# Attention values of two consecutive steps mixed together and summed in one PSUM bank

## The chip, the core and the metric

The kernel runs on one core of a Trainium2 chip. The metric is the device time of one execution in microseconds (us). Engines are named as the profile names them: PE is TensorE (its weight loads are PEld), DVE is VectorE, ACT is ScalarE, POOL is GpSimd, SP is SyncE. PE writes its results to PSUM, which has 8 banks; a bank holds 512 fp32 numbers for each of 128 partitions. DVE and ACT read PSUM, POOL does not.

## The reference

The program is a small network on 2 sequences of 1024 tokens with 256 features, all in fp32: a first attention with 16 heads of 16 features, a soft mixture of 64 experts, a rotation of the features, and two layers of a local-window attention with a gated feed-forward part. The change lies wholly in the first attention, which is this part of the reference:

```
qkv = (x @ Wqkv.T + bqkv).reshape(Bb, Ss, 3, H, HD).transpose(2, 0, 3, 1, 4)
q, k, v = (qkv[0], qkv[1], qkv[2])
attn = softmax(einsum('bhid,bhjd->bhij', q, k) / sqrt(HD), axis=-1)
...
out = einsum('bhij,bhjd->bhid', mod, v)       # mod is attn, gated and renormalised
```

For each of 2 x 16 heads, 1024 queries meet 1024 keys. The kernel computes exp(score - maximum), multiplies it with the values and with a column of ones (which gives the sum), and divides at the end.

## The kernel before

**Units and steps.** Four heads of one sequence form a unit; there are 8 units (`units`). A unit is worked off in 16 steps, 128 steps in all (`STEPS`). Step s belongs to unit s // 16, to one half n of the queries (512) and to one block j of 128 keys: j runs from 0 to 7, then n changes. Three kinds of work make up the loop at L767:

- `maxima(step, half)` (L301): the maximum of each query over the keys must be known before its exponentials. For two heads at a time ("half" 0 and 1), two matmuls with 32 contraction rows each fill a tile `pm` of two banks, and DVE reduces it to maxima (L317). This runs `LEAD` = 12 steps ahead of the scores, so that there are maxima for steps 12 to 127 in loop steps 0 to 115 and none in the last 12 loop steps. `largest` and `shift` turn the maxima of 8 steps around and put them into the queries (`qs`) of the next half unit.
- `score(step, half)` (L336): two matmuls with 32 contraction rows give the scores of two heads, each in a bank of its own (`sc`), and ACT takes the exponential into an SBUF tile `e` (L352). In the last 12 steps half 1 uses one tile of two banks and one exponential.
- `mix(s)` (L355): four matmuls, one a head, with 128 contraction rows (keys) and 32 output rows each, multiply the values `v` of step s with the four exponentials. The four results stand one under the other in one bank, `po`. For j = 0 ACT copies `po` to an SBUF tile `ob` (L373). For the other j the result is added to `ob`: ACT copies `po` to `part` (L379) and POOL adds (L380), or, from step 116 on, DVE adds straight from PSUM (L376).

An fp32 matmul is two passes, so that one matmul of the program is two MATMUL records of the profile: a loop step has 8 records of scores, 8 of maxima and 8 of mixing. The four matmuls of a mix lie in four column strips of the array and run side by side. Scores and maxima lie in four row strips: the scores of one half and the maxima of the other half run side by side.

**Order of the work.** PE, DVE and ACT take their instructions in the order in which the program is written here (`manual_schedule`). A loop step is: `largest` (on some even steps), the mix of two steps earlier, `shift` and the list `between` (on odd steps only: projections, transposes and the like), then score half 0 with maxima half 1, maxima half 0 with score half 1, and last the list `aside` (small DVE work). This document calls the two score-and-maxima pairs of one step its *block*.

**PSUM.** The 8 banks are two pools. `ps_s` has two buffers of two banks; in the loop only `pm` uses them (and, in the last 12 steps, the wide score tile). So the `pm` of a step can be written once DVE has reduced the `pm` of the same place in the step before. `ps_t` has four buffers of one bank, taken in turn by `po`, the four `sc` of a step, and whatever `between` needs. The exponentials `e` have 6 buffers, two a step.

At the end, `mix(126)` and `mix(127)` are written into the beginning of the next stage, after its first logits.

Of the kernel before, what the change touches and what calls it, by code (L numbers as in the profile page):

```python
# [91 lines left out]
def tile_kernel(ctx: ExitStack, tc: tile.TileContext, a: dict, out: bass.AP):  # L92
    nc = tc.nc
# [51 lines left out]
    at = ExitStack()  # L145
# [21 lines left out]
    VW = HD0 + 1  # L167
    v = [at1.tile([P, 8, H0 * VW + 32 - VW], F32, name=f"v{b}") for b in range(B)]
# [18 lines left out]
    def single(name):  # L187
        return ps_t[0].tile([P, 512], F32, tag="t", name=name)
# [130 lines left out]
    def largest(hu):  # L319
        mx2 = mxs.pop(hu)  # L320
        nc.vector.tensor_tensor(mxt[hu % 2][:, :, :, AUG], mx2[:, :, :, 0], mx2[:, :, :, 1], ALU.max)

    def shift(hu):

        u, n = divmod(hu, 2)
        pt = one("pmx")
        for i in range(4):
            nc.tensor.transpose(
                pt[:, i * P : (i + 1) * P], mxt[hu % 2][:, i, :, :].rearrange("p h r -> p (h r)"), ident
            )  # L330
        at = slice(n * 512, (n + 1) * 512)
        nc.vector.tensor_tensor(qs[u % 2][:, at], qm[u % 2][:, at], pt, ALU.add)

    es = {}

    def score(step, half):  # L336

        u, n, j = step // 16, step % 16 // 8, step % 8
        e = at2.tile([P, 2, 512], F32, tag="e", name="e", bufs=6)
        both = half and step >= STEPS - LEAD  # L340
        sc = wide("sc") if both else [single("sc") for x in range(2)]
        for x in range(2):
            r = slice(32 * (2 * half + x), 32 * (2 * half + x) + 32)
            nc.tensor.matmul(  # L344
                sc[:, x, :] if both else sc[x],
                km[u % 3][r, j * P : (j + 1) * P],
                qs[u % 2][r, n * 512 : (n + 1) * 512],
                start=True,
                stop=True,
            )  # L350
        for part, t in ((e, sc),) if both else ((e[:, x, :], sc[x]) for x in range(2)):
            nc.scalar.activation(part, t, AF.Exp, scale=1.0 / HD0**0.5)  # L352
        es[step, half] = e

    def mix(s):  # L355

        u, n, j = s // 16, s % 16 // 8, s % 8
        b, g = units[u]
        po = single("po")
        for hh in range(4):  # L360
            at = (4 * g + hh) * VW
            nc.tensor.matmul(  # L362
                po[32 * hh : 32 * hh + 32, :],
                v[b][:, j, at : at + 32],
                es[s, hh // 2][:, hh % 2, :],
                start=True,
                stop=True,
            )
        for x in range(2):
            es.pop((s, x))  # L370
        if j == 0:
            obs[u, n] = at2.tile([P, 512], F32, tag="ob", name=f"ob{u}_{n}")
            nc.scalar.copy(obs[u, n], po)  # L373
            return
        if s >= STEPS - LEAD:
            nc.vector.tensor_tensor(obs[u, n], obs[u, n], po, ALU.add)  # L376
            return
        part = at2.tile([P, 512], F32, tag="part", name="part", bufs=1)
        nc.scalar.copy(part, po)  # L379
        nc.gpsimd.tensor_tensor(obs[u, n], obs[u, n], part, ALU.add)  # L380
# [34 lines left out]
    def add_field(b, n, which=range(4)):  # L415
        o_tm = o_tms[b]
        for i in (4 * n + y for y in which):
            nc.vector.scalar_tensor_tensor(
                o_tm[:, i, :], sv[b], fac[:, b * 8 + i : b * 8 + i + 1], o_tm[:, i, :], ALU.mult, ALU.add
            )  # L420
# [27 lines left out]
    def out_by_token(b, n):  # L448
        for i in range(4):
            t0 = 1 + (4 * n + i) * P  # L450
            if i % 2 == 0:
                pt = one("pxt").rearrange("p (y d) -> p y d", d=D)
            for c in range(2):
                nc.tensor.transpose(pt[:, i % 2, c * P : (c + 1) * P], xa[:, c, b, t0 : t0 + P], ident)
            if i % 2:
                i0 = b * 8 + 4 * n + i - 1
                nc.vector.tensor_copy(xo_tm[:, i0 : i0 + 2, :], pt)
# [4 lines left out]
    STEPS = 16 * len(units)  # L462
# [253 lines left out]
    def of_banks(bufs):  # L716
        banks.close()
        ahead.clear()
        single_banks[0] = bufs == 4
        ps_t[0] = banks.enter_context(tc.tile_pool(name="ps_t", bufs=bufs, space=PSUM))  # L720
# [10 lines left out]
    for u in range(len(units)):  # L731
        if u % 2 == 0 and u + 2 < len(units):
            b, g = units[u + 2]
# [30 lines left out]
    with tc.manual_schedule(  # L764
        engines={mybir.EngineType.PE, mybir.EngineType.DVE, mybir.EngineType.Activation}
    ):
        for s in range(STEPS):  # L767
            u, p = s // 16, s % 16 // 2
            new = p in (3, 7) and s // 8 + 1 < 2 * len(units)
            if new and s % 2 == 0:  # L770
                largest(s // 8 + 1)
            if s >= 2:
                mix(s - 2)
            if s % 2:
                if new:
                    shift(s // 8 + 1)
                for f in between.get((u, p), ()):
                    f()
            m = s + LEAD
            for what in (0, 1) if m < STEPS else (0,):  # L780

                for f, step in ((score, s), (maxima, m))[:: 1 - 2 * what]:
                    if step < STEPS:
                        f(step, what if f is score else 1 - what)
            if m >= STEPS:
                score(s, 1)
            for f in aside.get(s, ()):
                f()
# [18 lines left out]
    def logits(it):  # L807

        n, m = divmod(it, 8)
        lg = wide("lg")  # L810
        for b in (1, 0):
            for k in range(2):
                nc.tensor.matmul(  # L813
                    lg[:, b, :],
                    xa[:, k, b, 1 + m * P : 1 + (m + 1) * P],
                    phi[:, k, n * 512 : (n + 1) * 512],
                    start=(k == 0),
                    stop=(k == 1),
                )
        keep = dx0.tile([P, B, 512], F32, tag="keep", name="keep")  # L820
        nc.scalar.copy(keep[:, 1, :], lg[:, 1, :])  # L821
        l1 = dx0.tile([P, 512], F32, tag="l1", name="l1")
        nc.vector.tensor_tensor(l1, lg[:, 0, :], keep[:, 1, :], ALU.subtract)  # L823
        nc.vector.tensor_copy(keep[:, 0, :], lg[:, 0, :])
        for b in range(B):
            nc.sync.dma_start(lgd[b * 8 + m][:, n * 512 : (n + 1) * 512], keep[:, b, :])
        dsps[it] = dx0.tile([P, B, 512], F32, tag="dsp", name="dsp")
        nc.scalar.activation(dsps[it][:, 0, :], l1, AF.Sigmoid)
        nc.scalar.activation(dsps[it][:, 1, :], l1, AF.Sigmoid, scale=-1.0)

    def dispatch(it):

        n, m = divmod(it, 8)
        if m == 0:
            accs[n] = [pair(f"sl{b}") for b in range(B)]
        d = dsps.pop(it)
        for b in range(B):
            for c in range(2):
                nc.tensor.matmul(  # L839
                    accs[n][b][:, c, :],  # L840
                    xo_tm[:, b * 8 + m, c * P : (c + 1) * P],
                    d[:, b, :],
                    start=(m == 0),
                    stop=(m == 7),
                )
        if m == 7:
            slots[n] = dx.tile([P, 2, B, 512], F32, tag="slots", name="slots", bufs=1)
            nc.scalar.copy(slots[n][:, :, 0, :], accs[n][0])
            nc.vector.tensor_copy(slots[n][:, :, 1, :], accs[n][1])
# [110 lines left out]
    with tc.manual_schedule(  # L960
        engines={mybir.EngineType.PE, mybir.EngineType.DVE, mybir.EngineType.Activation}
    ):
        logits(0)
        out_by_token(1, 0)
        mix(STEPS - 2)
        mix(STEPS - 1)
        of_banks(2)
        logits(1)
        by_token(len(units) - 1, 1)
        dispatch(0)  # L970
        add_field(1, 1)
        to_features(1, 1)
        logits(2)
        dispatch(1)
        project_out(1, 1)
        logits(3)
        dispatch(2)
        out_by_token(1, 1)
# [6 lines left out]
    y = [mo1.tile([P, NE // 4, D], F32, name="y0"), xp.tile([P, NE // 4, D], F32, tag="y1", name="y1")]  # L985
# [106 lines left out]
    with tc.manual_schedule(  # L1092
# [10 lines left out]
        ts, nrqs, vs, es, eTs, pos, oTs, hcs, us = {}, {}, {}, {}, {}, {}, {}, {}, {}  # L1103
# [455 lines left out]
        for s in range(-2, WINDOWS):  # L1559
# [73 lines left out]
            if s == 5:  # L1633

                f = xp.tile([P, 4 * NS], F32, tag="e", name="f")
                at = 0
# [159 lines left out]
```

## Time and profile before

| | us |
|---|---|
| median of 3 timed runs (1587.48 to 1588.11) | 1587.85 |
| span of the profiled execution, first to last instruction | 1586.1 |
| the same execution: time outside the span | not in the profile |
| loop step 0 begins (first score) | 63.2 |
| last mix ends, about | 499.6 |
| busy PE / DVE / ACT / POOL, whole span | 1572.0 / 904.2 / 892.3 / 538.6 |

The profile has a page of totals and groups, and a trace that can be asked for a list of instructions in order of time, for groups of instructions, for waits, and for the chain of work that ended last. In the list in order of time, a row has start, duration, engine, line, operation, tiles, shape, how many instructions are merged into the row, and in brackets the idle time of that engine before it and what ended it. A duration of a merged row runs from its first start to its last end. The ends of matmuls are modelled and overlap the next ones, so that the pace of PE is read from the starts. A wait that the profile puts down to an engine that had long been done was another's.

### The profile page before, as it was taken

The numbers are of one execution on the slowest core, as the hardware profiler recorded it, in microseconds if no ns is written. First come the engines' busy times: TensorE is split into PE (matmuls) and PEld (weight loads), VectorE is DVE, ScalarE is ACT, GpSimd is POOL, SyncE is SP. The second block draws the span as 40 slices with busy tenths as digits, with TensorE's granted clock in tenths as the row PEclk, the third lists the DMA queues.
The fourth block names the chain that finished last, engine by engine and source line by source line (L and its number), as shares of the span: only waits on it lengthen the run. The fifth ranks groups of instructions, "written<-read, shape, count | busy, mean of one in ns | idle before, by whom it ended". The sixth has DMA issues, their size and how long they took to land.

```text
span 1586.1 us, 22717 instructions
## 1 busy us (share of the span) xinstructions
PE 1572.0 (99%) x8672; PEld 801.4 (51%) x8672; DVE 904.2 (57%) x1606; ACT 892.3 (56%) x1678; POOL 538.6 (34%) x835
## 2 busy tenths in 40 slices
PE   8999999999999999999999999999999999999999
PEld 4333433333333444444887676555555555556554
DVE  5868768776863122225446656756565656656532
ACT  2578778787885222235234544666666565666641
POOL 3333323333330100000103444655554555465411
PEclk9999999999999999999999999999999999999999
DMA  5100010000000644546642002000100001000001
GB/s 161 54 15 13 1 21 8 8 14 8 1 1 34 172 152 139 184 149 185 204 130 77 30 1 82 1 1 1 67 1 0 14 1 56 1 11 17 14 14 40
DMA packets 49852, 82.66 MB, mean 52 GB/s; under 512 B 4552, under 2 KB 25200, under 8 KB 49488
## 3 DMA queue, kind: packets, MB, share of 16 engines
q1 hardware_dynamic: 47200, 75.38, 15.5%
q0 software_dynamic: 1584, 5.29, 1.1%
q8 instruction: 68, 1.11, 0.3%
q10 hardware_dynamic: 960, 0.56, 0.1%
q14 instruction: 40, 0.33, 0.1%
HBM read 56.04 MB, written 20.97 MB: 49 GB/s over the span
## 4 chain that ended last, share of the span: by engine, by line
PE 98%; DVE 1%; DMA 1%; ACT 0%; POOL 0%; issue 0%; ACTq 0%; DVEq 0%; POOLq 0%
PE sc L344 9%; PE pga L1412 9%; PE po L362 8%; PE pm L310 7%; PE lg L813 7%; PE pq L1140 7%; PE sl L839 7%; PE cmb L928 7%; PE py L1439 4%; PE po L1323 4%; PE sc L1243 4%; PE pwo L1343 3%; PE pe L1304 3%; PE pv L1210 3%; PE pqk L280 2%; PE py L860 2%
## 5 line engine op out<-in xcount | busy, mean ns | idle before, releaser
L317 DVE TENSOR_REDUCE mx<-pm 128x2 f32<-128x1024 f32 x256 | 301.6, 1220 | 108.0 <-PE pm L310 107.9
L352 ACT ACTIVATE e<-sc 128x512 f32<-128x512 f32 (+1 forms) x500 | 263.6, 613 | 67.7 <-PE pm L310 63.5
L344 PE MATMUL sc<-qs,km 32*128 32x512 f32 x1024 | 247.7, 616 | 0.7 <-ACT cg L562 0.7
L310 PE MATMUL pm<-km,qm 32*128 32x512 f32 x1024 | 242.8, 616 | 0.0
L380 POOL TENSOR_TENSOR ob<-ob,part 128x512 f32<-128x512 f32 x101 | 128.5, 1272 | 251.2 <-ACT part L379 251.2
L1412 PE MATMUL pga<-hc,w 128*128 128x512 f32 x320 | 141.8, 593 | 0.0
L1293 POOL TENSOR_SCALAR e<-e,den 128x256 f32<-128x256 f32 (+1 forms) x128 | 130.8, 1035 | 29.4 <-DVE den L1289 29.4
L362 PE MATMUL po<-e,v 128*32 128x512 f32 x1024 | 136.8, 604 | 0.0
L344 PEld LDWEIGHTS sc<-qs,km 32*128 32x128 f32 x1024 | 91.5, 183 | 86.6 <-ACT e L352 65.2
L1178 POOL TENSOR_TENSOR t<-raw,tabs 128x512 f32<-128x512 f32 x64 | 80.7, 1281 | 152.4 <-ACT raw L1170 147.2
L1277 ACT ACTIVATE e<-e,nmx 128x256 f32<-128x256 f32 (+1 forms) x256 | 123.5, 487 | 2.7 <-DVE nmx L1260 2.5
L1140 PE MATMUL pq<-wqo,xa 128*128 128x512 f32 x256 | 115.9, 595 | 1.1 <-ACT xa L955 0.7
L928 PE MATMUL cmb<-xb,y 128*128 128x256 f32 x512 | 116.5, 380 | 0.2 <-ACT xb L914 0.2
L813 PE MATMUL lg<-phi,xa 128*128 128x512 f32 x256 | 116.1, 595 | 0.0
L839 PE MATMUL sl<-dsp,xb 128*128 128x512 f32 x256 | 114.9, 592 | 0.0
L310 PEld LDWEIGHTS pm<-km,qm 32*128 32x128 f32 x1024 | 83.2, 183 | 49.3 <-DVE mx L317 35.0
L1260 DVE CUSTOM_DVE_ANT_0 e<-sc,mask,zn 128x256 f32<-128x256 f32 (+1 forms) x256 | 102.0, 463 | 6.3 <-PE sc L1243 6.3
L823 DVE TENSOR_TENSOR l<-lg,keep 128x512 f32<-128x512 f32 x32 | 22.1, 692 | 144.8 <-ACT keep L821 144.8
L928 PEld LDWEIGHTS cmb<-xb,y 128*128 128x128 f32 x512 | 95.0, 190 | 16.2 <-issue 2.8
L1170 ACT COPY raw<-pq 128x1024 f32<-128x1024 f32 x32 | 32.4, 1013 | 108.0 <-PE pq L1140 100.0
L1412 PEld LDWEIGHTS pga<-hc,w 128*128 128x128 f32 x320 | 59.0, 190 | 66.6 <-issue 64.3
L821 ACT COPY keep<-lg 128x512 f32<-128x512 f32 x32 | 18.7, 585 | 126.0 <-issue 105.3
(225 smaller groups left out, 2460.5 us busy)
## 6 DMA issues: line engine op xcount, KB each, us to landing
lgd<-keep SPq DMA_DIRECT2D x64, 256.0 KB, 2.4
w<-in_ffn_W SPq DMA_DIRECT2D x16, 1024.0 KB, 7.0
ebig<-lgd SPq DMA_DIRECT2D x64, 256.0 KB, 3.3
wqo<-in_wqkv SPq DMA_DIRECT2D x2, 1536.0 KB, 8.0
w<-in_w SPq DMA_DIRECT2D x2, 1386.0 KB, 5.9
km<-hk SPq DMA_DIRECT2D x32, 64.0 KB, 2.3
qm<-hq SPq DMA_DIRECT2D x32, 64.0 KB, 2.3
phi<-in_phi SPq DMA_DIRECT2D x1, 2048.0 KB, 7.7
```

The costliest lines, as they stand in the source:

```text
L310: nc.tensor.matmul(pm[:, x, :], qm[u % 2][r, i * P : (i + 1) * P], km[u % 3][r, n * 512 : (n + 1) * 512], start=True, stop=True,)
L317: nc.vector.tensor_reduce(mxs[hu][:, i % 4, 2 * half : 2 * half + 2, n], pm, AX.X, ALU.max)
L344: nc.tensor.matmul(sc[:, x, :] if both else sc[x], km[u % 3][r, j * P : (j + 1) * P], qs[u % 2][r, n * 512 : (n + 1) * 512], start=True, s ...
L352: nc.scalar.activation(part, t, AF.Exp, scale=1.0 / HD0**0.5)
L362: nc.tensor.matmul(po[32 * hh : 32 * hh + 32, :], v[b][:, j, at : at + 32], es[s, hh // 2][:, hh % 2, :], start=True, stop=True,)
L380: nc.gpsimd.tensor_tensor(obs[u, n], obs[u, n], part, ALU.add)
L813: nc.tensor.matmul(lg[:, b, :], xa[:, k, b, 1 + m * P : 1 + (m + 1) * P], phi[:, k, n * 512 : (n + 1) * 512], start=(k == 0), stop=(k == 1),)
L839: nc.tensor.matmul(accs[n][b][:, c, :], xo_tm[:, b * 8 + m, c * P : (c + 1) * P], d[:, b, :], start=(m == 0), stop=(m == 7),)
L928: nc.tensor.matmul(acs[q][:, c, :], y[b][:, 4 * jj + j, c * P : (c + 1) * P], eT[:, j // 2, j % 2 * 256 : (j % 2 + 1) * 256], start=(jj == ...
L1140: nc.tensor.matmul(pq[:, x, :], shifted(xa, k, b, w * WIN, P), load["wqkv"][:, k, x * 512 : (x + 1) * 512], start=(k == 0), stop=(k == 1),)
L1293: engine.tensor_scalar(e[:, x, c, lo:], e[:, x, c, lo:], den[:, x, c : c + 1], None, ALU.mult)
L1412: nc.tensor.matmul(pt[:, x, :], load["w1"][:, k, lo : lo + P], hcs[f][:, k, :], start=(k == 0), stop=(k == 1))
```

## The change

`mix(s)` is called for an even s only, in the odd loop step s + 3, and handles steps s and s + 1: eight matmuls instead of four, of which the second four add to the first four in the same bank (`start` only for the first step, `stop` for the second). One copy, or one copy and one addition, then serves both steps. Even loop steps have no mix. The line numbers after L358 grow by one.

```diff
         po = single("po")
-        for hh in range(4):
-            at = (4 * g + hh) * VW
-            nc.tensor.matmul(
-                po[32 * hh : 32 * hh + 32, :],
-                v[b][:, j, at : at + 32],
-                es[s, hh // 2][:, hh % 2, :],
-                start=True,
-                stop=True,
-            )
-        for x in range(2):
-            es.pop((s, x))
+        for y in range(2):
+            for hh in range(4):
+                at = (4 * g + hh) * VW
+                nc.tensor.matmul(
+                    po[32 * hh : 32 * hh + 32, :],
+                    v[b][:, j + y, at : at + 32],
+                    es[s + y, hh // 2][:, hh % 2, :],
+                    start=(y == 0),
+                    stop=(y == 1),
+                )
+            for x in range(2):
+                es.pop((s + y, x))
         if j == 0:
...
             if new and s % 2 == 0:
                 largest(s // 8 + 1)
-            if s >= 2:
-                mix(s - 2)
+            if s >= 3 and s % 2:
+                mix(s - 3)
             if s % 2:
...
         mix(STEPS - 2)
-        mix(STEPS - 1)
         of_banks(2)
```

## The prediction

> **What bounds the kernel now.** I read the page's totals first, then its groups, then the list in order of time at two places in the loop, then the chain that ended last.
>
> ```profile
> PE 1572.0 (99%) x8672; PEld 801.4 (51%) x8672; DVE 904.2 (57%) x1606; ACT 892.3 (56%) x1678; POOL 538.6 (34%) x835
> ...
> PE 98%; DVE 1%; DMA 1%; ACT 0%; POOL 0%; issue 0%; ACTq 0%; DVEq 0%; POOLq 0%
> ...
> L317 DVE TENSOR_REDUCE mx<-pm 128x2 f32<-128x1024 f32 x256 | 301.6, 1220 | 108.0 <-PE pm L310 107.9
> ```
>
> PE is busy 99% and makes 98% of the chain, so the time is PE's. But busy time is modelled, and what paces PE must be read from its starts. DVE's reductions are the next thing to look at: 256 of 1.22 us, two a loop step, each waiting for PE. The ordinary loop, from the list in order of time (from the mix of step 19 to that of step 20):
>
> ```profile
> 133.62 1.06 PE L362 MATMUL po<-e,v 128*32 128x512 f32 x8
> 134.62 0.70 PE L344 MATMUL sc<-qs,km 32*128 32x512 f32 x2
> ...
> 135.35 0.19 PEld L310 LDWEIGHTS pm<-km,qm 32*128 32x128 f32 x2 [0.42 <-DVE mx L317]
> ...
> 135.88 2.36 DVE L317 TENSOR_REDUCE mx<-pm 128x2 f32<-128x1024 f32 x2 [0.42 <-PE pm L310]
> ...
> 136.55 1.06 PE L362 MATMUL po<-e,v 128*32 128x512 f32 x8
> ```
>
> A mix takes 1.00 us to the next start (133.62 to 134.62), a block of scores and maxima 1.93 (to 136.55), a step 2.93. The mix of step 21 starts at 139.47, so that two steps are 5.85. DVE starts on a block's maxima 1.26 after the block begins and needs 2.36 for its two tiles: it ends 3.62 after the block's start. The second `pm` of the next block needs the buffer that is freed then. The next block starts at 2.93 and wants that buffer 0.97 into it (134.62 to 135.59 is the start of its second half), at 3.90. So the slack against DVE is only 0.3 us, less the load's own lead, and the mix is what provides it. The row at 135.35 shows that this load was released by DVE.
>
> Now a place where the loop of before has no mix between two blocks: steps 0 and 1, since the mix begins at step 2.
>
> ```profile
> 63.22 0.70 PE L344 MATMUL sc<-qs,km 32*128 32x512 f32 x2 [0.70 <-ACT cg L562]
> ...
> 64.48 4.81 DVE L317 TENSOR_REDUCE mx<-pm 128x2 f32<-128x1024 f32 x4 [1.43 <-PE pm L310]
> ...
> 65.03 0.29 PEld L344 LDWEIGHTS sc<-qs,km 32*128 32x128 f32 x2 [0.64 <-ACT e L352]
> ...
> 65.52 0.29 PEld L344 LDWEIGHTS sc<-qs,km 32*128 32x128 f32 x2 [0.20 <-ACT e L352]
> ...
> 66.89 0.19 PEld L310 LDWEIGHTS pm<-km,qm 32*128 32x128 f32 x2 [0.83 <-DVE mx L317]
> ...
> 67.96 1.06 PE L362 MATMUL po<-e,v 128*32 128x512 f32 x8
> ```
>
> Step 0's block starts at 63.22, step 1's at 65.03, 1.82 later. Its second score waits for a `sc` bank until 65.52, and its second `pm` waits for DVE until 66.89. DVE began at 63.22 + 1.26, as in the ordinary loop, and ended those two tiles at + 3.62; PE went on 0.05 later. The mix comes at 67.96: two blocks back to back take 4.74, not twice 1.93. This is the pattern that the change makes of every pair of steps.
>
> **The change part by part.**
>
> *Work removed.* ACT's copies to `part` fall from 101 to 43 (58 x 0.59 = 34 us), POOL's additions likewise (58 x 1.27 = 74 us), DVE's additions at L376 from 11 to 5 (6 x 0.69 = 4 us). Matmuls, exponentials, reductions and every DMA keep their number. I cost the removed work at nothing: it lies beside PE. ACT idles 63.5 us before its exponentials, waiting for PE, and what waited for `part` or for `ob` on PE are a handful of rows of up to 0.8 us, the length that PE also shows at each change from blocks to mixes. It also buys nothing at the wait above, which is on DVE's reductions, and those have 1201 to 1226 ns throughout, whatever POOL does beside them.
>
> *Mixes joined.* Within one kind of work a pass follows the last by 0.43 (eight passes of the projection in 3.44). Two passes of a mix should take 0.86 and take 1.00; four of a block should take 1.72 and take 1.93. So a change of kind and back costs 0.14 + 0.21, by finer starts 0.34 a step, and an even step without a mix saves it. Where two mixes stand together today, after the loop, the chain shows what a joined one costs:
>
> ```profile
> 482.42 1.00 PE po L362 x8
> ...
> 497.84 1.85 PE po L362 x16
> ```
>
> That is 1.85. Summing in PSUM costs no extra: the coherence product at L552 sums eight matmuls in the same four column strips at 0.43 to 0.45 a pass.
>
> The Trainium skill's "TensorEngine Tiling (Array Packing)" says in its section on tiling modes that a change of mode drains the array. By that rule alone the change would remove a drain pair from 57 even steps, and with the 0.34 of the rows the sum would be -19 us. Its section on the PSUM bottleneck warns the other way, that packed matmuls outrun what empties PSUM, but gives no price. The rows at 63 to 68 us decide between the two.
>
> *The cover that is lost.* With the mix gone from the even step, PE reaches that step's second `pm` at 1.82 + 0.86 = 2.68 after the odd block's start, and DVE frees it at 3.62 + 0.05 = 3.67. Once it is freed, 1.07 pass until the next mix (66.89 to 67.96). Unstalled, two blocks would be 1.82 + 1.93 - 0.11 (no change of kind before the second) = 3.64; they are 4.74. The stall is 1.10 us. What queues behind the waiting load on PE are the two scores of half 1 and then the joined mix; nothing on PE can pass it. ACT then gets half 1's scores late and idles, which costs nothing more: the next block's scores reuse banks whose exponentials ended long before.
>
> *Sum for a pair.* 1.85 + 4.74 = 6.59 against 5.85: +0.74, which is -0.34 for the changes of kind and +1.10 for the stall, within rounding. It holds for even steps 4 to 114, 56 of them, because in every odd step before 116 DVE starts at 1.26 and ends at 3.62, whatever stands in `between` (that is ahead of the block, and DVE's small work there ends before 1.26). 56 x 0.74 = 41.4. In the next odd block nothing is late: DVE ended 69.29 - 63.22 = 6.07 after the pair's first block, 1.8 before it is needed again. The `po` bank is reused by the last score of the odd block; today the copy starts 0.19 after the block (134.81 against 134.62), lasts 0.59, and that score starts at 0.98, so this stays as it is.
>
> *Step 2.* Blocks 0, 1 and 2 now follow each other. Block 2's second `pm` waits for DVE's 69.29; with 0.05 and 1.07 the joined mix starts at 70.41 and ends at 72.26. Today the mix of step 1 starts at 70.89 and ends at 71.89. +0.4.
>
> *The last twelve steps.* There are no maxima, so no DVE stall. Today a step is about 2.07 (mixes at 463.27 and 465.34). A joined mix needs the exponentials of the odd step two before, with one block between: they end about 3.2 after their scores, and PE is there at 1.93. The mix's first half covers 0.86 of that. I estimate 4.2 a pair against 4.13, and at the step that carries a `shift` a gain, since today's mix at 467.47 stretches to 1.39. Bounds for six pairs: -2 (PE alone, 3.78 a pair) and +5 (0.8 more wait each). I take 0, near which both estimates lie.
>
> *Waits that could be new.* `e` has 6 buffers; step s writes what step s - 3 left, whose mix still precedes step s's scores on PE. No new wait. `by_token` and `gate_outputs` read `ob` two or more steps after its last mix, as before. SP's and POOL's DMA issues are not moved past anything.
>
> *Total.* 41.4 + 0.4 + 0 = 41.8 on the span of 1586.1: 1627.9. The profile gives no time outside the span; the median 1587.85 stands 1.75 above it, and I keep that: **1629.7 us**, +2.6%.
>
> **The rivals.**
>
> 1. *The changes of kind decide* (other side, faster). If DVE's tile were free in time, 57 x -0.34 = -19 us, 1568. For it: PE is 99% busy, and its busy time falls. Against it: steps 0 and 1 show the stall itself. It decides only if DVE ended a block's maxima 1.0 us sooner, at 2.6; two reductions of 1.22 after 1.26 cannot. 5%, with all that lies between no change and it.
> 2. *More is late than in steps 0 and 1.* These had no copy of `po` on ACT and no bank taken by `po`. If the copy delayed the odd block's last score by its whole length, 0.59 a pair, 57 of them would add 34: 1663. Against it is the timing of the copy above. 8%, mostly for smaller amounts of the same kind.
> 3. *The change does little*: the stall and the saving cancel because other waits in the ordinary loop already contain the stall. The ordinary loop's block is 1.93 in all but three steps, so there is none to cancel. 2%.
>
> **How the numbers follow.** The case above has 85%. Its own range: 0.70 to 0.79 a pair gives 39 to 44, the tail -2 to +5: 1625 to 1637. Rival 2's smaller amounts reach up, a partly hidden stall down; I give 1620 to 1640 for eight in ten. A change under 0.2% (3.2 us), about what a measurement of this kernel can tell, counts as the same. Faster 5%: rival 1. Same 2%: rival 3. Slower 93%.
>
> **What the profile after would show.** Mixes as rows of 16 records, 1.85 to the next start, 6.59 apart where `between` is empty. In every even step a PE load of `pm` released by DVE, with about 0.8 idle before it, and DVE's reductions in runs of four, 4.8 long. `part` copies 43. PE's matmul groups unchanged in number. The waits of `pm` on DVE grow from 30 us to some 60 or more. Everything after 540 us is the old profile moved by about 42 us. The prediction is wrong if even blocks take 1.8 to 2.0 us, or if the stall sits elsewhere, on `sc` behind ACT.

## The result and the profile after

The changed kernel takes 1628.48 us (median of 4 runs, 1628.01 to 1629.06), beside 1587.98 for the kernel before (1587.48 to 1588.25). The ratio is 1.0257, with a 95% interval of 1.0244 to 1.0271. That is slower by 40.5 us; 1629.7 was predicted. The profiled execution of the changed kernel took 1628.86 us, its span 1626.7, so 2.2 us lie outside it.

Four lines of the page after: engines with their busy time, the shares of the chain that ended last, and two groups (out<-in, count | busy us, mean ns | idle before, and what ended it).

```profile
PE 1612.5 (99%) x8672; PEld 834.3 (51%) x8672; DVE 900.3 (55%) x1600; ACT 869.9 (53%) x1620; POOL 465.5 (29%) x777
...
PE 98%; DVE 1%; DMA 0%; ACT 0%; POOL 0%; issue 0%; ACTq 0%; DVEq 0%; POOLq 0%
...
L317 DVE TENSOR_REDUCE mx<-pm 128x2 f32<-128x1024 f32 x256 | 301.5, 1219 | 126.1 <-PE pm L310 123.3
...
L381 POOL TENSOR_TENSOR ob<-ob,part 128x512 f32<-128x512 f32 x43 | 54.5, 1267 | 257.8 <-ACT part L380 257.8
```

POOL lost 73 us of busy time and ACT 22, and the time did not fall by any of it. PE issues the same 8672 matmul records, yet its "busy" time rose by 40.5. The page alone would read as if the matmuls had become longer. The list in order of time shows what happened. This is one pair of steps after, from an odd block (140.90) to the next joined mix (145.64):

```profile
140.90 0.70 PE L344 MATMUL sc<-qs,km 32*128 32x512 f32 x2
...
141.09 0.59 ACT L380 COPY part<-po 128x512 f32<-128x512 f32 x1 [0.85 <-PE po L363]
...
142.16 2.35 DVE L317 TENSOR_REDUCE mx<-pm 128x2 f32<-128x1024 f32 x2 [1.59 <-PE pm L310]
...
142.71 0.29 PEld L344 LDWEIGHTS sc<-qs,km 32*128 32x128 f32 x2 [0.64 <-ACT e L352]
...
144.57 0.19 PEld L310 LDWEIGHTS pm<-km,qm 32*128 32x128 f32 x2 [0.83 <-DVE mx L317]
...
144.61 2.36 DVE L317 TENSOR_REDUCE mx<-pm 128x2 f32<-128x1024 f32 x2
...
145.64 1.92 PE L363 MATMUL po<-e,v 128*32 128x512 f32 x16
```

DVE begins 1.26 after the odd block (142.16), and the even block's second `pm` load is released 3.67 after it (144.57), after 0.83 of idle weight loads whose end the profile puts down to DVE. The mix follows 1.07 later. The mix before this one started at 139.04, so a pair is 6.60 long. Measured step by step from the first score record of each step:

| | before | after | difference |
|---|---|---|---|
| ordinary odd step to even step | 2.925 | 1.821 | -1.10 |
| ordinary even step to the next odd step | 2.925 | 4.774 | +1.85 |
| the pair | 5.850 | 6.595 | +0.745 |
| step 0 to step 3 | 9.25 | 9.64 | +0.39 |
| step 0 to step 115 | 396.05 | 438.08 | +42.03 |
| step 115 to step 127 | 32.92 | 32.43 | -0.49 |
| start of step 0 in the span | 63.22 | 62.29 | -0.93 |

The last three rows sum to +40.6, which is the difference of the spans.

### The profile page after: what moved, and what is told of

Its sections match the earlier page's. It is cut to its first block, busy times and chain, and to the rows that moved or that the text cites. A ratio compares the mean times of both kernels' runs of the same rounds, so it can differ in the third digit from the quotient of the medians.

```text
span 1626.7 us, 22545 instructions
## 1 busy us (share of the span) xinstructions
PE 1612.5 (99%) x8672; PEld 834.3 (51%) x8672; DVE 900.3 (55%) x1600; ACT 869.9 (53%) x1620; POOL 465.5 (29%) x777
## 4 chain that ended last, share of the span: by engine, by line
PE 98%; DVE 1%; DMA 0%; ACT 0%; POOL 0%; issue 0%; ACTq 0%; DVEq 0%; POOLq 0%
PE pm L310 10%; PE sc L344 9%; PE pga L1412 8%; PE po L363 7%; PE lg L814 7%; PE pq L1140 7%; PE sl L840 7%; PE cmb L929 6%; PE py L1439 4%; PE po L1323 4%; PE sc L1243 4%; PE pwo L1343 3%; PE pe L1304 3%; PE pv L1210 3%; PE pqk L280 2%; PE py L861 2%
## 5 line engine op out<-in xcount | busy, mean ns | idle before, releaser
L317 DVE TENSOR_REDUCE mx<-pm 128x2 f32<-128x1024 f32 x256 | 301.5, 1219 | 126.1 <-PE pm L310 123.3
L344 PE MATMUL sc<-qs,km 32*128 32x512 f32 x1024 | 276.2, 625 | 0.7 <-ACT cg L563 0.7
L310 PE MATMUL pm<-km,qm 32*128 32x512 f32 x1024 | 259.4, 627 | 0.2
L344 PEld LDWEIGHTS sc<-qs,km 32*128 32x128 f32 x1024 | 104.3, 183 | 83.6 <-ACT e L352 61.0
L381 POOL TENSOR_TENSOR ob<-ob,part 128x512 f32<-128x512 f32 x43 | 54.5, 1267 | 257.8 <-ACT part L380 257.8
L363 PE MATMUL po<-e,v 128*32 128x512 f32 x1024 | 124.8, 599 | 0.0
L310 PEld LDWEIGHTS pm<-km,qm 32*128 32x128 f32 x1024 | 79.1, 183 | 69.8 <-DVE mx L317 51.9
```

The lines of the kernel that those rows point to most:

```text
L310: nc.tensor.matmul(pm[:, x, :], qm[u % 2][r, i * P : (i + 1) * P], km[u % 3][r, n * 512 : (n + 1) * 512], start=True, stop=True,)
L317: nc.vector.tensor_reduce(mxs[hu][:, i % 4, 2 * half : 2 * half + 2, n], pm, AX.X, ALU.max)
L344: nc.tensor.matmul(sc[:, x, :] if both else sc[x], km[u % 3][r, j * P : (j + 1) * P], qs[u % 2][r, n * 512 : (n + 1) * 512], start=True, s ...
L363: nc.tensor.matmul(po[32 * hh : 32 * hh + 32, :], v[b][:, j + y, at : at + 32], es[s + y, hh // 2][:, hh % 2, :], start=(y == 0), stop=(y ...
```

## Experiments

Two questions were put. Is the loss the stall on DVE's reductions, or the way in which two mixes share a bank? And what would be left if the stall were gone? My theory was that putting two blocks back to back makes PE wait for DVE. The rivals were that the shared bank or the copies delay something, and that without DVE's wait the saved changes of kind would make the kernel faster.

### The move without the sum in PSUM

Both mixes stand in the odd step, but each has its own bank, its own copy and its own addition, as before.

```diff
-            if s >= 2:
+            if s >= 3 and s % 2:
+                mix(s - 3)
                 mix(s - 2)
...
-        part = at2.tile([P, 512], F32, tag="part", name="part", bufs=1)
+        if s % 2:
+            part = dx0.tile([P, B, 512], F32, tag="keep", name="part1")[:, 0, :]
+        else:
+            part = at2.tile([P, 512], F32, tag="part", name="part", bufs=1)
```

> The kernel before, in which the mixes of two steps stand one after the other in every second step, as in the changed kernel, but in two PSUM banks, each with its own copy and addition: only the move, without the sum in PSUM. Theory: the place of the mixes is all that counts. PE's order is that of the changed kernel, the two copies fit beside it, and the time is that of the changed kernel, 1628 (1626 to 1631). Rival A (summing in one bank costs PE time, for example by waiting for the first sum): clearly faster than the changed kernel. Rival B (the copies and additions saved are worth something): slower than the changed kernel, up to 58 x 0.59 = 34 us.

Measured: 1630.35 us (1629.75 to 1631.07), ratio 1.0269 [1.0253, 1.0284], inside the expected range. One pair of this kernel, from the list in order of time (the last row is cut by the window after 12 of its 16 records):

```profile
139.22 1.92 PE L362 MATMUL po<-e,v 128*32 128x512 f32 x16
...
140.41 0.59 ACT L382 COPY part<-po 128x512 f32<-128x512 f32 x1
141.26 0.59 ACT L382 COPY part<-po 128x512 f32<-128x512 f32 x1 [0.27 <-PE po L362]
141.40 2.60 POOL L383 TENSOR_TENSOR ob<-ob,part 128x512 f32<-128x512 f32 x2
...
144.74 0.19 PEld L310 LDWEIGHTS pm<-km,qm 32*128 32x128 f32 x2 [0.83 <-DVE mx L317]
...
145.81 1.50 PE L362 MATMUL po<-e,v 128*32 128x512 f32 x12
```

There are two copies and two additions again, and the pair is 6.59 long (139.22 to 145.81), with the same 0.83 of idle ended by DVE. The move makes the whole loss. The sum in PSUM and the saved copies are worth at most about 2 us over the kernel. By the traces, 0.24 of that has gathered by step 115 and 1.0 more by step 125; there two blocks take 3.52 (519.71 to 523.23) instead of 2.31 (519.70 to 522.01), and a load of the scores is released by DVE's addition at L376.

### DVE's reductions cut to half

Only half of each `pm` tile is reduced. The matmuls and their order stay as they are after.

```diff
-        nc.vector.tensor_reduce(mxs[hu][:, i % 4, 2 * half : 2 * half + 2, n], pm, AX.X, ALU.max)
+        nc.vector.tensor_reduce(mxs[hu][:, i % 4, 2 * half : 2 * half + 2, n], pm[:, :, :256], AX.X, ALU.max)
```

> The changed kernel, in which each reduction of the maxima reads only the first 256 of the 512 columns of a head: half of the maxima's DVE work is left out, all matmuls stay. From the rows of the kernel before (0.41 us for 256 elements a partition, 1.22 for 1024) a reduction of 512 should take about 0.68. Theory (DVE's hold on the maxima tiles makes the stall): the second tile of an even step comes free at 2.6 instead of 3.67, and what is late next is the second score's bank at 2.30, behind ACT. By the rows of a pair that gives the joined mix at about 4.24 instead of 4.74 after the odd block's start, a pair of 6.09, and 57 x 0.50 = 29 us less: 1600 (1596 to 1604). Rival A (ACT's hold on the score banks makes the whole stall): no change, 1628. Rival B (the maxima tiles are all of it, nothing behind them): a pair of 5.5, 1568.

Measured: 1604.8 us (1604.26 to 1605.53), ratio to before 1.0108 [1.0091, 1.0125]. The direction is as expected: 24 of the 40 us went with DVE's time. But 1600 was forecast, with 1604 as its upper end, and what is late next had been mis-named. The list in order of time, over the same pair (the last row is cut likewise):

```profile
136.76 0.70 PE L344 MATMUL sc<-qs,km 32*128 32x512 f32 x2
...
137.92 3.04 ACT L352 ACTIVATE e<-sc 128x512 f32<-128x512 f32 x6 [0.38 <-PE pm L310]
138.03 1.46 DVE L317 TENSOR_REDUCE mx<-pm 128x2 f32<-128x512 f32 x2 [2.36 <-PE pm L310]
...
139.54 0.24 PEld L310 LDWEIGHTS pm<-km,qm 32*128 32x128 f32 x2 [0.18 <-DVE mx L317]
...
140.03 0.70 PE L344 MATMUL sc<-qs,km 32*128 32x512 f32 x2
140.03 0.30 PEld L344 LDWEIGHTS sc<-qs,km 32*128 32x128 f32 x3
...
141.09 1.50 PE L363 MATMUL po<-e,v 128*32 128x512 f32 x12
```

DVE is done 2.73 after the block's start (139.49), not 3.62. Yet the mix comes 4.33 after it (136.76 to 141.09), where two unstalled blocks would be 3.64. ACT works through the four exponentials of the odd block from 137.92. The fourth stands alone in a narrow window of the list:

```profile
139.37 0.62 ACT L352 ACTIVATE e<-sc 128x512 f32<-128x512 f32 x1
```

It ends at 139.99, 3.22 after the block's start. The load of the even block's last score, whose bank it held, comes 0.05 later (among those at 140.03), and 1.06 after it the mix. The fourth `sc` bank is late, not the second. So with DVE relieved the pair is 1.82 + 4.36 = 6.18, still 0.33 longer than before.

### DVE's reductions cut to three quarters

If ACT's fourth bank is now the last, DVE may take longer again without any cost, as long as its bank comes free before 3.27, where the load of the last score came with the half.

```diff
-        nc.vector.tensor_reduce(mxs[hu][:, i % 4, 2 * half : 2 * half + 2, n], pm, AX.X, ALU.max)
+        nc.vector.tensor_reduce(mxs[hu][:, i % 4, 2 * half : 2 * half + 2, n], pm[:, :, :384], AX.X, ALU.max)
```

> The changed kernel, in which each reduction reads 384 of the 512 columns of a head (a quarter of the maxima's DVE work is left out). By the rows for 512 and 1024 elements a reduction of 768 takes 0.95 and the second tile comes free at about 3.13 after the odd block's start. Theory (with 256 columns the fourth score bank, held by ACT until 3.27, had become the last wait): 3.13 is still earlier than that, so the time is the same as with 256 columns, 1604.8 (1603.5 to 1606). Rival (DVE still was the last wait with 256 columns): the time lies half way between 1604.8 and 1628.5, at 1616.

Measured: 1605.2 us (1604.91 to 1605.65), ratio 1.0112 [1.0098, 1.0126], the time of the half within the runs' spread. The list in order of time (the last row again cut):

```profile
137.39 0.70 PE L344 MATMUL sc<-qs,km 32*128 32x512 f32 x2
...
138.55 3.05 ACT L352 ACTIVATE e<-sc 128x512 f32<-128x512 f32 x6 [0.38 <-PE pm L310]
138.65 1.82 DVE L317 TENSOR_REDUCE mx<-pm 128x2 f32<-128x768 f32 x2 [1.89 <-PE pm L310]
...
140.53 0.19 PEld L310 LDWEIGHTS pm<-km,qm 32*128 32x128 f32 x2 [0.54 <-DVE mx L317]
140.66 0.70 PE L344 MATMUL sc<-qs,km 32*128 32x512 f32 x2
140.66 0.30 PEld L344 LDWEIGHTS sc<-qs,km 32*128 32x128 f32 x3
...
141.72 1.49 PE L363 MATMUL po<-e,v 128*32 128x512 f32 x12
```

DVE now ends 0.35 later (3.08 after the block's start), its wait is named again with 0.54 of idle, and still the last score comes 3.27 after the block's start and the mix 4.33 after it, both as with the half. The wait that a row names is not the one that sets the time here. DVE's is hidden under ACT's. That it is ACT's rests on these rows and on the equal times; no run made the exponentials shorter.

### The same cut in the kernel before

```diff
-        nc.vector.tensor_reduce(mxs[hu][:, i % 4, 2 * half : 2 * half + 2, n], pm, AX.X, ALU.max)
+        nc.vector.tensor_reduce(mxs[hu][:, i % 4, 2 * half : 2 * half + 2, n], pm[:, :, :256], AX.X, ALU.max)
```

> The kernel before, with the same shortened reductions (half of the maxima's DVE work is left out). Theory: in the kernel before PE has slack against DVE in every step, the single mix provides it, so nothing moves but three steps with small waits: 1587 (1586.5 to 1588). Rival: if DVE's reductions were a cost in the kernel before as well, it gains with the shorter ones, as the changed kernel does, by 10 us or more.

Measured: 1587.3 us (1586.28 to 1587.76, 10 runs), ratio 0.9997 [0.9988, 1.0007]. From the page of this kernel, the group of the reductions:

```profile
L317 DVE TENSOR_REDUCE mx<-pm 128x2 f32<-128x512 f32 x256 | 175.9, 691 | 211.6 <-PE pm L310 202.0
```

126 us less of DVE's work (175.9 instead of 301.6) bring nothing while a mix stands between the blocks. The same cut brings 24 us when it does not. One stretch of this kernel's loop did move: from step 0 to step 3, the one place where blocks stand back to back here too, 9.25 became 8.83, and every other step kept its length to 0.02. The reduction itself is not expensive; it becomes so by the order.

### The other work moved into the even steps

If the loss is lost cover, other PE work between the two blocks should bring it back. Here the lists of other work (`between`) stand in the even steps, where there is now no mix.

```diff
-            if s % 2:
-                if new:
-                    shift(s // 8 + 1)
+            if s % 2 and new:
+                shift(s // 8 + 1)
+            if s % 2 == (s >= STEPS - LEAD):
                 for f in between.get((u, p), ()):
                     f()
```

> The changed kernel, in which the lists of other work (projections, transposes; not the turning of the maxima) run in the even steps, ahead of their blocks, instead of in the odd steps, up to step 115. Theory: any PE work between two blocks covers the stall. 31 odd steps have such a list, of 0.59 to 3.69 us; the sum of the smaller of 1.10 and the list's length is 26 us, less about 0.2 for changes of kind at the 16 long ones: 23 us less, 1605 (1601 to 1609). Rival (the stall is not between two blocks, but in the joined mix or behind ACT): no change, 1628, or slower by the added changes of kind.

Measured: 1614.56 us (1612.75 to 1615.23), ratio 1.0167 [1.0152, 1.0182]. That is 14 us less than after, as the theory has it in sign, but 9.6 more than expected. By the traces, steps 0 to 127 are 15.6 shorter than after, where 23 was forecast. Most of the difference, 5.4, lies in four lists that hold work tied to DVE: their pairs were to gain 3.4 and lost 1.9. The other 2.0 are small sums at many lists, where the changes of kind were mis-sized: most lists of 0.59 gained 0.52, and a pair with a long list came to 9.34 instead of 10.23, a gain of 0.88 where 0.90 was counted, or of 0.69 where a `shift` stays in the odd step. What is left of the 9.6 lies outside the loop, 1.3 of it in the loop's start (63.57 in this run, 62.29 after). Steps 74 and 75 show one of the four lists, in the list in order of time:

```profile
310.19 0.47 DVE L419 SCALAR_TENSOR_TENSOR o_tm<-sv,fac,o_tm 128x256 f32<-128x256 f32 x1
...
310.71 0.53 PEld L430 LDWEIGHTS poT<-ident,o_tm 128*128 128x128 f32 x5 [1.82 <-DVE o_tm L419]
311.41 0.70 PE L344 MATMUL sc<-qs,km 32*128 32x512 f32 x2
...
313.34 1.92 PE L363 MATMUL po<-e,v 128*32 128x512 f32 x16
```

The transposes at L430 need `o_tm`, which DVE writes after the odd block's reductions. Placed in the even step they wait for those reductions themselves, 1.82 of idle, and the pair is 8.54 long where it is 7.62 after. Work that depends on DVE is no cover for DVE.

### The same, with those four lists left where they were

This builds on the kernel of the section above.

```diff
-            if s % 2 == (s >= STEPS - LEAD):
+            late = s >= STEPS - LEAD or (u, p) in ((4, 2), (4, 5), (6, 2), (6, 5))
+            if s % 2 == late:
```

> The experiment with lists in even steps, but four lists stay in odd steps: the two that turn values which DVE has only just finished (steps 69 and 75), and the two that give DVE two copies ahead of its reductions (steps 101 and 107). In the trace of that experiment these four pairs took 0.82, 0.92, 0.06 and 0.15 us more than in the changed kernel. Theory (a list covers the gap unless it waits for DVE or holds DVE up itself): 1.9 us less than with all lists moved, 1612.6 (1612 to 1613.5). Rival (lists cover badly for a reason of their own): no change from 1614.6.

Measured: 1611.17 us (1610.93 to 1611.51), ratio 1.0149 [1.0133, 1.0164]. Steps 0 to 127 take 452.99 in the trace, where the kernel above has 454.93: -1.94, as expected (1.9). The median is 0.8 below the expected range, though: the medians differ by 3.4. The other 1.5 lie outside the loop: in the profiled executions the loop starts 1.0 earlier (62.56 instead of 63.57), ahead of everything in which the two kernels differ, and the runs of the kernel above spread over 2.5.

### Joined only where a list covers the gap

Twelve pairs are joined: seven of the ordinary loop whose list of other work needs nothing from DVE, and five of the last steps, which have no maxima. In those seven of the ordinary loop the list goes into the even step. The two mixes after the loop are summed too, as in the changed kernel. Everywhere else the mixes and the lists stand as in the kernel before.

```diff
-    def mix(s):
+    def mix(s, both=True):
...
-        for y in range(2):
+        for y in range(1 + both):
...
-                    stop=(y == 1),
+                    stop=(y == both),
...
+    JOINED = (9, 37, 41, 43, 73, 85, 91, 119, 121, 123, 125, 127)
...
-            if s >= 3 and s % 2:
+            joined = (s | 1) in JOINED
+            if joined and s % 2:
                 mix(s - 3)
-            if s % 2:
-                if new:
-                    shift(s // 8 + 1)
+            if not joined and s >= 2:
+                mix(s - 2, False)
+            if s % 2 and new:
+                shift(s // 8 + 1)
+            if s % 2 == (not joined or s >= STEPS - LEAD):
```

> Two steps are mixed together only where something covers the gap: in seven pairs whose list of other work is long and waits for nothing on DVE (it runs in the even step, as in the experiment with lists in even steps), and in the last 12 steps, which have no maxima. All other steps are mixed one by one, as in the kernel before. Theory: in those seven pairs the experiment with lists in even steps took 0.14 to 0.18 us less than the kernel before (for example 5.56 + 3.78 against 2.93 + 6.56), 1.0 in all, and from step 117 to 127 the changed kernel took 0.9 less. Together 1.9 us less than before, 1585.7 (1585.0 to 1586.5). Rival (the joined mix never pays, its gain at the changes of kind is eaten by something not seen): 1587.6 or more.

Measured: 1585.71 us (1584.92 to 1587.4, 11 runs), beside 1587.61 for the kernel before (15 runs): ratio 0.9989 [0.998, 0.9998]. This is 0.1% less than the kernel before, with an interval that only just leaves out 1 and a difference below the 0.2% that the prediction took as the least that counts; the trace has to show where it lies. Steps 7 to 9, PE alone, in order of time. Before:

```profile
88.23 0.70 PE L344 MATMUL sc<-qs,km 32*128 32x512 f32 x2
...
90.16 1.07 PE L362 MATMUL po<-e,v 128*32 128x512 f32 x8
91.16 0.70 PE L344 MATMUL sc<-qs,km 32*128 32x512 f32 x2
...
93.09 1.07 PE L362 MATMUL po<-e,v 128*32 128x512 f32 x8
94.08 3.70 PE L280 MATMUL pqk<-xT,w_att 128*128 128x512 f32 x8
97.72 0.70 PE L344 MATMUL sc<-qs,km 32*128 32x512 f32 x2
```

And joined, with the projection in the even step:

```profile
88.13 0.70 PE L344 MATMUL sc<-qs,km 32*128 32x512 f32 x2
...
90.06 3.70 PE L280 MATMUL pqk<-xT,w_att 128*128 128x512 f32 x8
93.69 0.70 PE L344 MATMUL sc<-qs,km 32*128 32x512 f32 x2
...
95.62 1.92 PE L363 MATMUL po<-e,v 128*32 128x512 f32 x16
97.47 0.70 PE L344 MATMUL sc<-qs,km 32*128 32x512 f32 x2
```

The projection takes 3.63 of PE between the blocks, more than the stall needs, so that the even block after it runs at its own 1.93 (93.69 to 95.62). The joined mix is 1.85 where the two single ones are 1.00 and 0.99. The pair, from the scores of step 7 to those of step 9, is 9.34 (88.13 to 97.47) instead of 9.48 (88.23 to 97.72). Over the loop, steps 0 to 116 are 1.24 shorter and steps 0 to 127 are 1.90 shorter. The seven pairs make 1.05 of that, as forecast. Another 0.23 fall in a pair that is not joined (steps 105 to 107), whose cause stays open. The last steps give 0.65 where 0.9 was forecast, and one pair (steps 123 to 125) gives all of it; the other joins there gain nothing. So the total came out as forecast in part by luck.

## Why the prediction was right

**The pair.** It was put at 6.59 and measured 6.595; its two parts, the two blocks and the joined mix, at 4.74 + 1.85 and measured 4.74 (140.90 to 145.64) + 1.86 (139.04 to 140.90). The pattern of steps 0 and 1 before is the pattern of every ordinary pair after. Steps 0 to 115 were put at +41.8 and came to +42.03, step 2's share at +0.4 and came to +0.39.

**The cause.** That DVE's drain of `pm` is the wait is shown from two sides: the same cut of DVE's work is worth 24 us after and nothing before, but for the one place before that has the new order. Why the cut does not bring back all 40 is told below. That the shared bank and the copies do not matter is shown by the move without the sum. What was costed at nothing, the removed work of ACT and POOL, is worth at most 2 us.

**The copy of `po` (rival 2).** It runs at 141.09, 0.19 after the odd block begins, as it did before, and delays nothing: the odd step to even step is 1.821, which is what steps 0 and 1 had without any copy.

**The changes of kind.** The 0.34 is real where nothing waits. At one place in the last steps, from mix to mix over two blocks with no list, 4.14 before (461.20 to 465.34) became 3.78 after (503.97 to 507.75). At the next such place it is 4.19 before (470.44 to 474.63) and 4.15 after (512.68 to 516.83), for the joined mix stretches while it waits for exponentials. The Trainium skill's "TensorEngine Tiling (Array Packing)", section on tiling modes, says that a change of mode drains the array, and the first of these places fits it, with 0.36 a pair; the rows show the time, not the drain itself. The rule did not decide: in an ordinary pair the stall of 1.10 stands against what it saves.

**Where it was off.** Three terms were missed. Two of them, -0.49 and -0.93, with +0.2 more than forecast in the loop, let the sum come out 1.2 high.

- *The last twelve steps* were taken as 0 and came to -0.49, inside the bounds given, but by luck, since it is a sum of unlike parts: +0.46 from step 115 to 117, -0.26 in the pair with the `shift`, -0.69 from step 123 to 125, and nothing in the other three pairs. Of the -0.69, 0.42 is one place: behind the `pot` transposes, the scores of a step took 0.80 more than usual before (478.41 to 480.28 is 1.87, others 1.07); after, two blocks there take 2.31 (519.70 to 522.01), 0.38 more than the usual 1.93.
- *The start of the loop* came 0.93 earlier, which no step of the prediction foresaw. It lies ahead of everything that the change touches. Six of the traces have the same work ahead of the loop (before, after, and the kernels with mixes moved, lists moved, four lists left and twelve pairs joined), and their loops start between 62.18 and 63.57; the latest and the third earliest of these starts belong to kernels that differ only in where four lists stand, far behind the start. So 0.93 is within what the start scatters by, and that this term helped the sum is chance.
- *The waits* of `pm` loads on DVE were to grow "from 30 us to some 60 or more". The 30 held for 50 to 430 us only. The view of the reductions, in the part on who waited for them, first before and then after (us, times):

```profile
  PEld pm L310: 35.0, 78
```

```profile
  PEld pm L310: 51.9, 64
```

The sum of waits rose by 17 us while the loop lost 42. Fewer loads wait, each for longer, and the idle put down to a load is less than what it delays: 0.83 in the row at 144.57, for a stall of 1.10. The growth of a wait in this view is not the growth of the time.

**What the argument left out.** Rival 1 said that the changes of kind would make the kernel faster, 1568, if DVE ended a block's maxima 1.0 sooner, at 2.6. With the half tile DVE ended at 2.73, 0.13 short of that, and the kernel was still 1.1% slower than before, and with three quarters, at 3.08, just as slow. The condition was incomplete. Behind DVE's bank stands ACT's fourth `sc` bank, free at 3.27, and it alone keeps a pair 0.33 longer than before. I had taken it that half 1's scores getting late "costs nothing more", which holds while DVE is later, but not once it is relieved. So the predicted case was even safer than I argued.

**What stays open.** Summing two mixes in PSUM without moving them was not tried: a bank would have to stay open over a whole step, and the four single banks are all in use. That DVE must drain the odd block before the even block can end, since four halves in a row need four `pm` tiles and there are two, is argued from the order of the program; the half tile shows only that its duration counts. That ACT's fourth bank sets the time once DVE is relieved is read from the rows, as said above.

## What to carry to other kernels

Work that stands between two bursts of matmuls may be what gives other engines time to empty PSUM, even where PE shows 99% busy. Before gathering such work, look in the profile for a place that already has the new order, and read its starts there. Gathering pays where something independent of the draining engine fills the gap, as in the seven pairs of the ordinary loop here, and even there only by 0.14 to 0.18 us a pair. And when one wait is taken away, work out the release time of every bank behind it, not only that of the next one.

## What the runs showed of the hardware

- DVE's maximum over a PSUM tile took 691 ns for 512 numbers a partition, 953 for 768 and 1219 for 1024: about 1.03 ns a number and 0.16 us besides. POOL's load beside it changed nothing (1200 to 1226 ns with 58 POOL additions fewer, 1201 to 1226 with them).
- A waiting weight load followed the end of the work that released it by about 0.05 us, for ACT's exponentials as for DVE's reductions.
- With two banks late at nearly the same time, the idle row named DVE (0.54 of idle) although ACT's bank, 0.13 later, set the time; the load for ACT's bank showed no idle row of its own.
